# Selective scan: which engine multiplies by B and by C, and where dA and the states lie

## The chip, the core and the metric

The kernel runs on one core of one Trainium2 chip. The metric is the device time of one execution in microseconds (us). Five engines work side by side, each on its own in-order queue of instructions: PE (TensorE, matmuls; PEld is its weight load), DVE (VectorE), ACT (ScalarE), POOL (GpSimd) and SP (SyncE, which here issues all DMA transfers). An engine's instruction can wait for semaphores that other engines' instructions raise; whatever is queued behind it on the same engine waits too. SBUF is the on-chip working memory, PSUM the memory into which TensorE writes.

## The reference, cut to what matters

The input x is two images of 96 channels by 128 x 128 pixels. A block of four selective scans (Mamba) over the pixels in four orders, a quantised feed-forward layer, a 3 x 3 convolution and a second feed-forward layer follow each other; the change touches only the scans. For each of four directions, with 192 inner channels and 16 states per channel:

```python
xz = x @ in_w.T;  xc, z = split(xz)
xc = silu(conv4(xc) + conv_b)                   # causal, 4 taps, per channel
dt_raw, Bm, Cm = split(xc @ xproj_w.T)          # 6, 16 and 16 columns
dt = softplus(dt_raw @ dt_w.T + dt_b)
A = -exp(A_log)
def step(h, t):                                 # over 16384 positions
    dA = exp(dt_t[:, :, None] * A)
    h = dA * h + dt_t[:, :, None] * B_t[:, None, :] * u_t[:, :, None]
    y = einsum('bds,bs->bd', h, C_t)
    return h, y
y = (ys + Dp * xc) * silu(z)
out = y @ outp_w.T
```

## The kernel before, in words

For each of the two images (batches) `normalize` does a layer norm and writes the image to DRAM in row order (`xnr`) and column order (`xnc`), `mamba` does the four scans, and `ffn_and_conv` does the rest. Only `mamba` and the constants change.

`mamba` takes two directions at a time (a row order and a column order, forward for `pi` = 0 and backward for `pi` = 1), so that 2 x 192 = 384 channels fill three groups `g` of 128 partitions; group 1 holds 64 channels of each direction. Positions are cut into 32 pieces of T = 512. One pair of directions and one piece is a step: 2 x 32 = 64 steps per batch, 128 in all. In a step each group goes through the 16 states two at a time: 3 x 8 = 24 units (g, s) per step, 3072 in all.

A unit does this. TensorE broadcasts two rows of B over the partitions into the PSUM tile `bc` (L282, one-hot weights times three bf16 parts that sum to the float32 row). ScalarE makes `da` = exp(dt x A), one instruction per state (L285). VectorE multiplies dt x u (`dtu`) by the broadcast B inside `bc` (L290) and runs two scans h = da x h + b (L293), which start from the last states of the piece before, kept in `hst`. ScalarE copies the last columns of `h` to `hst` (L297). GpSimd multiplies `h` by two rows of C, `cs` (L299), which a DMA has broadcast from DRAM (`c_rows`, L274). TensorE adds the two products into the PSUM tile `y` by matmuls with an identity (L301).

After a group's eighth unit `finish` adds the skip Dp x xc to y on VectorE (L308), multiplies by the gate `sz` on GpSimd (L309), and behind groups 1 and 2 projects (L314 to L324) and adds the result to `acc`.

What a step needs beforehand is made during the step before by the generator `prologue`, one piece behind each unit from the third on: the loads of the input rows, the convolution folded into the input projection (L182), SiLU (L206, L211), the row products for C (L218, written to DRAM as `cd`) and for B and dt (L228), the split of B into bf16 parts, and for each group softplus in a numerically careful form: ScalarE |x|, relu(x), exp (L249 to L252), VectorE q (L255), ScalarE ln (L257), and on GpSimd q, ln, dt and dtu (L258 to L262).

The order on ScalarE's queue is the order in which the program is written (`manual_schedule`). On the other engines a scheduler orders the instructions when the program is built. Tiles come from pools with a fixed number of buffers; a tile that takes a buffer again waits for all readers of the tile that had it. PSUM holds two `bc` (two banks each), one `y` and three `misc`.

Of the kernel before, what the change touches and what calls it, by code (L numbers as in the profile page):

```python
# [1 line left out]

# [29 lines left out]
AHEAD = 3  # L32
DTO = 96
# [3 lines left out]
def tile_metaformer(ctx: ExitStack, tc: tile.TileContext, a: dict, out: bass.AP):  # L37
# [21 lines left out]
    bdw = const("bdw", (128, 2, NG, DTO + 2 * RK))  # L59
    cw = const("cw", (128, 2, NG, 2 * S))  # L60
    dtw = const("dtw", (2 * RK, 2, NG * 128))
    dtb = const("dtb", (128, 2, NG))
    dskip = const("dskip", (128, 2, NG))
# [4 lines left out]

    amat = cpool.tile([128, 2, NG, S], F32, name="amat")
    sel = cpool.tile([96, S, 2, 128], BF16, name="sel")  # L70
# [3 lines left out]
    with tc.tile_pool(name="prep", bufs=1) as pp, tc.tile_pool(name="prep_ps", bufs=2, space=PSUM) as pps:  # L74
# [4 lines left out]
        onehot = pp.tile([96, 2, S], F32, name="onehot")  # L79
        nc.sync.dma_start(onehot, a["onehot"])  # L80
        for d in range(2):
            nc.vector.tensor_copy(sel[:, :, d, :], onehot[:, d, :, None].broadcast_to((96, S, 128)))
# [75 lines left out]
    def mamba(acc, xnr, xnc):  # L158

        with ExitStack() as st:  # L160
            pool = lambda n, bufs, **kw: st.enter_context(tc.tile_pool(name=n, bufs=bufs, **kw))
            io, one, two, gen = pool("io", 2), pool("one", 1), pool("two", 2), pool("gen", 6)
            ps_bc, ps_y, ps_m = (pool(n, k, space=PSUM) for n, k in (("ps_bc", 2), ("ps_y", 1), ("ps_m", 3)))
# [21 lines left out]
            def prologue(pi, i, d):  # L185

                rev = pi == 1
                lo = L - (i + 1) * T if rev else i * T
                src = []
                for n, dram in (("xa", xnr), ("xb", xnc)):  # L190
                    t = io.tile([C, T + 3], F32, name=n)
                    if i == 0:
                        nc.gpsimd.memset(t[:, T : T + 3] if rev else t[:, 0:3], 0.0)
                        nc.sync.dma_start(t[:, 0:T] if rev else t[:, 3 : T + 3], dram[:, lo : lo + T])
                    else:
                        nc.sync.dma_start(t, dram[:, lo : lo + T + 3] if rev else dram[:, lo - 3 : lo + T])
                    src.append(t[:, ::-1] if rev else t)
                yield
                d["xc"], d["sz"], d["dt"], d["dtu"] = [], [], [], []
                ps = []  # L200
                for g in range(NG):
                    ps.append(inproj(pi, g, lambda dd, k, lo, hi: inx[:, dd, k, lo:hi], src, (0, 1, 2, 3)))
                    yield
                for g in range(NG):
                    xc = gen.tile([128, T], F32, name="xc")
                    nc.scalar.activation(xc, ps[g], AF.Silu, bias=convb[:, pi, g : g + 1])  # L206
                    d["xc"].append(xc)
                for g in range(NG):
                    z = inproj(pi, g, lambda dd, k, lo, hi: inz[:, dd, lo:hi], src, (3,))
                    sz = gen.tile([128, T], F32, name="sz", bufs=5)  # L210
                    nc.scalar.activation(sz, z, AF.Silu)  # L211
                    d["sz"].append(sz)
                nc.scalar.preload_act_table_set("natural_log_exp_and_others")
                yield

                ps = misc()
                for g in range(NG):
                    nc.tensor.matmul(ps[0 : 2 * S, :], cw[:, pi, g, :], d["xc"][g], start=g == 0, stop=g == NG - 1)  # L218
                crow = one.tile([2 * S, T], F32, name="crow")
                nc.scalar.copy(crow, ps[0 : 2 * S, :])  # L220
                d["cd"] = rows_d.tile([2 * S, T], F32, name="cd")
                nc.sync.dma_start(d["cd"], crow)
                yield


                ps = misc()
                for g in range(NG):
                    nc.tensor.matmul(ps[0 : DTO + 2 * RK, :], bdw[:, pi, g, :], d["xc"][g], start=g == 0, stop=g == NG - 1)  # L228
                parts = two.tile([96, T], BF16, name="parts")
                nc.scalar.copy(parts, ps[0:96, :])  # L230
                rest = one.tile([96, T], F32, name="rest")
                nc.vector.tensor_tensor(rest, ps[0:96, :], parts, ALU.subtract)
                dtr = one.tile([2 * RK, T], F32, name="dtr")
                nc.scalar.copy(dtr, ps[DTO : DTO + 2 * RK, :])
                yield
                mid = one.tile([96, T], BF16, name="mid")
                nc.gpsimd.tensor_copy(mid, rest)
                nc.vector.tensor_copy(parts[32:64, :], mid[32:64, :])
                nc.gpsimd.tensor_tensor(parts[64:96, :], rest[64:96, :], mid[64:96, :], ALU.subtract)
                d["parts"] = parts  # L240
                yield


                for g in range(NG):
                    ps = misc()
                    nc.tensor.matmul(ps, dtw[:, pi, g * 128 : (g + 1) * 128], dtr, start=True, stop=True)
                    bias = dtb[:, pi, g : g + 1]
                    e = one.tile([128, T], F32, name="e")
                    nc.scalar.activation(e, ps, AF.Abs, bias=bias)  # L249
                    dt = gen.tile([128, T], F32, name="dt", bufs=4)  # L250
                    nc.scalar.activation(dt, ps, AF.Relu, bias=bias)  # L251
                    nc.scalar.activation(e, e, AF.Exp, scale=-1.0)  # L252
                    yield
                    q = one.tile([128, T], F32, name="q")
                    nc.vector.tensor_scalar(q, e, 1.0, 1.0, ALU.add, ALU.subtract)  # L255
                    ln = one.tile([128, T], F32, name="ln")
                    nc.scalar.activation(ln, e, AF.Ln, bias=1.0)  # L257
                    nc.gpsimd.tensor_tensor(q, e, q, ALU.subtract)  # L258
                    nc.gpsimd.tensor_tensor(ln, ln, q, ALU.add)  # L259
                    nc.gpsimd.tensor_tensor(dt, dt, ln, ALU.add)  # L260
                    dtu = gen.tile([128, T], F32, name="dtu", bufs=4)
                    nc.gpsimd.tensor_tensor(dtu, dt, d["xc"][g], ALU.mult)  # L262
                    d["dt"].append(dt)
                    d["dtu"].append(dtu)
                    yield

            def c_rows(d, g, s):

                cs = gen.tile([128, 2, T], F32, name="cs", bufs=4)
                for half in range(2) if g == 1 else (slice(None),):  # L270
                    rows = slice(half * 64, half * 64 + 64) if g == 1 else half
                    at = s + S * (half if g == 1 else g // 2)
                    n = 64 if g == 1 else 128
                    nc.sync.dma_start(cs[rows], d["cd"][None, at : at + 2, :].broadcast_to((n, 2, T)))  # L274
                return cs

            def inputs_of(pi, d, g, s):

                bp = ps_bc.tile([128, 2, T], F32, name="bc")
                for j in range(2):  # L280
# [229 lines left out]
```

## Time and profile before

| | us |
|---|---|
| median of 3 runs | 18649.57 |
| lowest and highest | 18648.17 and 18655.98 |
| the profiled execution | 18639.52 |
| its span | 18637.7 |
| VectorE busy | 12812.0 (69%) |
| GpSimd busy | 10041.0 (54%) |
| ScalarE busy | 6766.3 (36%) |
| DMA, queue q1 | 1725.11 MB, 29.9% of 16 engines' time |
| TensorE's mean granted clock | 0.864 |

The profile page comes from one execution. Its groups name a line, an engine, an operation, out<-in, the shape and the count, then the busy time in us and the mean of one in ns, and behind the bar the idle time of the engine just before these instructions and what ended most of it. A line of waits reads: who waited, for whom, us in total, times, longest. A line of the timeline reads: start in us, duration in us, engine, line, operation, names, shape, count of merged instructions, and in brackets the idle time before. A line of stretches gives for each stretch the busy time of every engine with the number of instructions, the granted clock, the share of the DMA engines and GB/s.

### The profile page before, as it was taken

What the parts mean: (1) busy time and instruction counts of PE and PEld (TensorE: products, weight loads), DVE (VectorE), ACT (ScalarE), POOL (GpSimd) and SP (SyncE); (2) the same over time, 40 slices, a digit from 0 to 9 for tenths busy, and PEclk for the clock granted to TensorE, in tenths of its full rate; (3) what the DMA queues carried; (4) which work ended last, traced back from release to release, by engine and by line L of the source; (5) the groups of instructions that cost most, each with busy time, mean ns of one, the idle gap of its engine ahead of it and who ended that gap; (6) DMA issues with size and microseconds to landing.
All of it is one profiled execution on the core that took longest, in us unless ns stands there. A gap on an engine that the chain in (4) does not pass through costs nothing. (4 is left out here: it accounts for less than half of the span.)

```text
span 18637.7 us, 119806 instructions
## 1 busy us (share of the span) xinstructions
PE 14287.1 (77%) x33424; PEld 5080.7 (27%) x33424; DVE 12812.0 (69%) x12267; ACT 6766.3 (36%) x13205; POOL 10041.0 (54%) x5412
## 2 busy tenths in 40 slices
PE   6777777777777777777767777777787777777777
PEld 2222222222222222223322222222222222222233
DVE  4777777777777777753347777777777777777533
ACT  2433333343333433422223433333333334334222
POOL 2666666666666666630026666666666666666300
PEclk7888998899988888877778889988888888888777
DMA  2333333333333333310023333333333333333100
GB/s 87 109 105 108 108 107 108 105 108 108 107 106 106 106 106 106 107 55 6 6 85 106 108 106 108 108 107 106 106 107 107 104 107 106 108 106 106 54 6 6
DMA packets 511015, 1732.76 MB, mean 93 GB/s; under 512 B 75612, under 2 KB 76988, under 8 KB 505640
## 3 DMA queue, kind: packets, MB, share of 16 engines
q1 hardware_dynamic: 510344, 1725.11, 29.9%
q8 instruction: 263, 4.31, 0.1%
q14 instruction: 408, 3.34, 0.1%
HBM read 1678.68 MB, written 46.14 MB: 93 GB/s over the span
## 5 line engine op out<-in xcount | busy, mean ns | idle before, releaser
L299 POOL TENSOR_TENSOR hc<-h,cs 128x1024 f32<-128x1024 f32 x3072 | 7245.3, 2362 | 5219.9 <-DVE h L293 3434.5
L301 PE MATMUL y<-hc,ident 128*128 128x512 f32 x12288 | 7260.5, 722 | 2487.3 <-POOL hc L299 2456.2
L293 DVE TENSOR_TENSOR_SCAN h<-da,hst,bc 128x512 f32<-128x512 f32 x5952 | 7218.0, 1262 | 211.0 <-ACT da L285 72.9
L290 DVE TENSOR_TENSOR bc<-dtu,bc 128x1024 f32<-128x1024 f32 x3072 | 3685.8, 1219 | 2206.1 <-PE bc L282 2198.5
L301 PEld LDWEIGHTS y<-hc,ident 128*128 128x128 f32 x12288 | 2534.1, 224 | 6549.6 <-POOL hc L299 4297.4
L285 ACT ACTIVATE da<-dt,amat 128x512 f32<-128x512 f32 x6144 | 4080.7, 712 | 1.5
L297 ACT COPY hst<-h 128x2 f32<-128x2 f32 x3072 | 586.0, 191 | 7922.3 <-DVE h L293 7922.1
L282 PE MATMUL bc<-parts,sel 96*128 96x512 bf16 x6144 | 1970.8, 396 | 571.7 <-DVE h L293 568.4
L416 POOL TENSOR_TENSOR acc<-acc,y 96x512 f32<-96x512 f32 x128 | 147.0, 1148 | 2158.8 <-DVE y L415 2158.8
L282 PEld LDWEIGHTS <-sel 96*128 96x128 bf16 x6144 | 598.6, 102 | 2583.7 <-issue 2521.4
L182 PE MATMUL misc<-xa,inx 96*128 96x512 f32 (+1 forms) x2048 | 1054.8, 611 | 64.0 <-issue 32.2
L182 PE MATMUL misc<-xb,inx 96*64 96x512 f32 (+1 forms) x2048 | 1047.6, 610 | 0.3 <-ACT dt L251 0.3
L308 DVE SCALAR_TENSOR_TENSOR yg<-xc,dskip,y 128x512 f32<-128x512 f32 x384 | 285.3, 743 | 745.8 <-PE y L301 745.8
L309 POOL TENSOR_TENSOR yg<-yg,sz 128x512 f32<-128x512 f32 x384 | 485.5, 1264 | 543.9 <-DVE yg L308 486.8
L431 PE MATMUL pc<-pad,kw 96*96 96x512 f32 x1152 | 663.0, 699 | 48.2 <-DVE pad L129 48.2
L126 PE MATMUL pr<-sd,bcast_w 128*96 128x128 f32 x2048 | 450.1, 390 | 313.5 <-DVE sd L123 309.5
L114 ACT ACTIVATE sq<-xm 96x512 f32<-96x512 f32 x256 | 161.0, 629 | 1202.6 <-DVE xm L112 1161.1
L211 ACT ACTIVATE sz<-misc 128x512 f32<-128x512 f32 x384 | 229.3, 597 | 996.7 <-POOL yg L309 656.3
L260 POOL TENSOR_TENSOR dt<-dt,ln 128x512 f32<-128x512 f32 x384 | 490.9, 1278 | 20.2
L259 POOL TENSOR_TENSOR ln<-ln,q 128x512 f32<-128x512 f32 x384 | 485.5, 1264 | 30.1
L262 POOL TENSOR_TENSOR dtu<-dt,xc 128x512 f32<-128x512 f32 x384 | 486.6, 1267 | 27.8
L258 POOL TENSOR_TENSOR q<-e,q 128x512 f32<-128x512 f32 x384 | 484.7, 1262 | 9.6 <-DVE q L255 9.6
(88 smaller groups left out, 9731.6 us busy)
## 6 DMA issues: line engine op xcount, KB each, us to landing
cs<-cd SPq DMA_DIRECT2D x2048, 512.0 KB, 3.7
cs<-cd SPq DMA_DIRECT2D x2048, 256.0 KB, 3.9
xa<-xnr SPq DMA_DIRECT2D x124, 193.1 KB, 3.4
xb<-xnc SPq DMA_DIRECT2D x124, 193.1 KB, 4.0
acc<-in_x_dram SPq DMA_DIRECT2D x16, 768.0 KB, 16.2
xnr<-xn SPq DMA_DIRECT2D x16, 768.0 KB, 4.3
xnc<-st SPq DMA_DIRECT2D x16, 768.0 KB, 4.6
out_dram<-acc SPq DMA_DIRECT2D x64, 192.0 KB, 2.1
```

The costliest lines, as they stand in the source:

```text
L182: nc.tensor.matmul(ps[rows, :], w(PAIRS[pi][d], k, lo, hi), src[d][:, k : k + T], **se)
L259: nc.gpsimd.tensor_tensor(ln, ln, q, ALU.add)
L260: nc.gpsimd.tensor_tensor(dt, dt, ln, ALU.add)
L262: nc.gpsimd.tensor_tensor(dtu, dt, d["xc"][g], ALU.mult)
L282: nc.tensor.matmul(bp[:, j, :], w, d["parts"], start=True, stop=True)
L285: nc.scalar.activation(da[:, j, :], d["dt"][g], AF.Exp, scale=amat[:, pi, g, s + j : s + j + 1])
L290: nc.vector.tensor_tensor(bp, d["dtu"][g][:, None, :].broadcast_to((128, 2, T)), bp, ALU.mult)
L293: nc.vector.tensor_tensor_scan(h[:, j, :], da[:, j, :], bp[:, j, :], 0.0 if i == 0 else hst[:, g, s + j : s + j + 1], ALU.mult, ALU.add,)
L297: nc.scalar.copy(hst[:, g, s : s + 2], h[:, :, T - 1])
L299: nc.gpsimd.tensor_tensor(hc, h, cs, ALU.mult)
L301: nc.tensor.matmul(y, ident, hc[:, j, :], start=s + j == 0, stop=s + j == S - 1)
L431: nc.tensor.matmul(pc, kw[:, t, :], rows, start=t == 0, stop=t == 8)
```

## The change

B and C rows now come together. One row product (`bcw`) gives dt, B and C; `rows` writes the 64 rows of B and C, interleaved, to DRAM as `bcd`, and `bc_rows` broadcasts four rows (two of B, two of C) per unit by DMA into the SBUF tile `bc`, of which there are five buffers. GpSimd multiplies `dtu` into the B part of `bc`, two units ahead of the scan (L289). ScalarE writes `da` into PSUM (three buffers of two banks); the scans read it there and write the states back in its place (L300); ScalarE copies the last columns from there (L304), and VectorE multiplies the states by the C part of `bc` (L306). The skip becomes a matmul with a diagonal matrix `dmat` that opens the sum `y`; VectorE multiplies y by the gate. `misc` has one PSUM buffer instead of three. ScalarE takes the convolution and the gate out of PSUM as they are, and SiLU runs once over all three groups of each. The prologue's pieces stand at fixed units of the step before (`at`), and projection and collection two and three units behind a group's end.

```diff
-AHEAD = 3
-DTO = 96
+ROWS_AHEAD = 3
+AHEAD = 2
+BY_POOL = ()
+BCO = 32
+NBC = 4 * S
...
+        for pi in range(2):
+            for g in range(NG):
+                nc.vector.tensor_scalar_mul(dmat[:, pi, g, :], ident, dskip[:, pi, g : g + 1])
...
-            io, one, two, gen = pool("io", 2), pool("one", 1), pool("two", 2), pool("gen", 6)
-            ps_bc, ps_y, ps_m = (pool(n, k, space=PSUM) for n, k in (("ps_bc", 2), ("ps_y", 1), ("ps_m", 3)))
+            io, one, two, gen = pool("io", 2), pool("one", 1), pool("two", 2), pool("gen", 4)
+            ps_w, ps_y, ps_m = (pool(n, k, space=PSUM) for n, k in (("ps_w", 3), ("ps_y", 1), ("ps_m", 1)))
...
+                def conv(g):
+                    ps = inproj(pi, g, lambda dd, k, lo, hi: inx[:, dd, k, lo:hi], src, (0, 1, 2, 3))
+                    if g == 0:
+                        d["xc"] = two.tile([128, NG, T], F32, name="xc")
+                    nc.scalar.activation(d["xc"][:, g, :], ps, AF.Identity, bias=convb[:, pi, g : g + 1])
+
+                def gate(g):
+                    ps = inproj(pi, g, lambda dd, k, lo, hi: inz[:, dd, lo:hi], src, (3,))
+                    if g == 0:
+                        d["sz"] = two.tile([128, NG, T], F32, name="sz")
+                    nc.scalar.copy(d["sz"][:, g, :], ps)
+
+                def silu():
+                    for t in (d["xc"], d["sz"]):
+                        nc.scalar.activation(t, t, AF.Silu)
+                    nc.scalar.preload_act_table_set("natural_log_exp_and_others")
+
+                def rows():
+
+                    ps = misc()
+                    for g in range(NG):
+                        nc.tensor.matmul(
+                            ps[0 : BCO + NBC, :], bcw[:, pi, g, :], d["xc"][:, g, :], start=g == 0, stop=g == NG - 1
+                        )
+                    d["rows"] = one.tile([BCO + NBC, T], F32, name="rows")
+                    nc.scalar.copy(d["rows"], ps[0 : BCO + NBC, :])
+                    d["bcd"] = rows_d.tile([NBC, T], F32, name="bcd")
+                    nc.sync.dma_start(d["bcd"], d["rows"][BCO:, :])
...
+                def dt_in(g):
+                    ps = misc()
+                    nc.tensor.matmul(ps, dtw[:, pi, g * 128 : (g + 1) * 128], d["rows"][0 : 2 * RK, :], start=True, stop=True)
...
+                    nc.scalar.activation(d["e"], ps, AF.Abs, bias=bias)
...
+                    nc.scalar.activation(dt, ps, AF.Relu, bias=bias)
+                    nc.scalar.activation(d["e"], d["e"], AF.Exp, scale=-1.0)
...
+                def dt_ln(g):
+                    d["q"] = one.tile([128, T], F32, name="q")
+                    nc.vector.tensor_scalar(d["q"], d["e"], 1.0, 1.0, ALU.add, ALU.subtract)
+                    d["ln"] = one.tile([128, T], F32, name="ln")
+                    nc.scalar.activation(d["ln"], d["e"], AF.Ln, bias=1.0)
+
+                def dt_q(g):
+                    nc.gpsimd.tensor_tensor(d["q"], d["e"], d["q"], ALU.subtract)
+
+                def dt_log(g):
+                    nc.gpsimd.tensor_tensor(d["ln"], d["ln"], d["q"], ALU.add)
+
+                def dt_sum(g):
+                    nc.gpsimd.tensor_tensor(d["dt"][g], d["dt"][g], d["ln"], ALU.add)
+
+                def dt_u(g):
+                    dtu = gen.tile([128, T], F32, name="dtu")
+                    nc.gpsimd.tensor_tensor(dtu, d["dt"][g], d["xc"][:, g, :], ALU.mult)
...
+                at = [(0, load), (9, silu), (10, rows)]
+                at += [(k, partial(conv, g)) for g, k in enumerate((2, 3, 4))]
+                at += [(k, partial(gate, g)) for g, k in enumerate((5, 6, 8))]
+                for g, k in enumerate((11, 14, 18)):
+                    for m, f in ((0, dt_in), (1, dt_ln), (2, dt_q), (3, dt_log), (3, dt_sum), (4, dt_u)):
+                        at.append((k + m, partial(f, g)))
+                return sorted(at, key=lambda p: p[0])
+
+            def bc_rows(d, g, s):
+
+                bc = gen.tile([128, 2, 2, T], F32, name="bc", bufs=5)
...
+                    src = d["bcd"][None, at : at + 4, :].broadcast_to((n, 4, T))
+                    nc.sync.dma_start(bc[rows].rearrange("p s k t -> p (s k) t"), src)
+                return bc
+
+            def inputs_of(pi, d, g, s, bc):
+
+                b = bc[:, :, 0, :]
+                nc.gpsimd.tensor_tensor(b, d["dtu"][g][:, None, :].broadcast_to((128, 2, T)), b, ALU.mult)
+                da = ps_w.tile([128, 2, T], F32, name="da")
                 for j in range(2):
                     nc.scalar.activation(da[:, j, :], d["dt"][g], AF.Exp, scale=amat[:, pi, g, s + j : s + j + 1])
-                return bp, da
+                return da
+
+            def scans(i, d, g, s, bc, da):
+                b, c = bc[:, :, 0, :], bc[:, :, 1, :]
+                by_pool = (g, s) in BY_POOL
+                h = b if by_pool else da
                 for j in range(2):
                     nc.vector.tensor_tensor_scan(
-                        h[:, j, :], da[:, j, :], bp[:, j, :],
+                        h[:, j, :], da[:, j, :], b[:, j, :],
                         0.0 if i == 0 else hst[:, g, s + j : s + j + 1], ALU.mult, ALU.add,
                     )
                 nc.scalar.copy(hst[:, g, s : s + 2], h[:, :, T - 1])
-                hc = two.tile([128, 2, T], F32, name="hc")
-                nc.gpsimd.tensor_tensor(hc, h, cs, ALU.mult)
+                if not by_pool:
+                    nc.vector.tensor_tensor(c, h, c, ALU.mult)
+
+            def sums(s, y, bc):
                 for j in range(2):
-                    nc.tensor.matmul(y, ident, hc[:, j, :], start=s + j == 0, stop=s + j == S - 1)
+                    nc.tensor.matmul(y, ident, bc[:, j, 1, :], start=False, stop=s + j == S - 1)
...
+            def gated(pi, d, g, y):
                 t = one.tile([128, T], F32, name=f"yg{g}")
...
+                nc.vector.tensor_tensor(t, y, d["sz"][:, g, :], ALU.mult)
...
+            for k in range(total + 4):
+                n, u = divmod(k, nu)
+                if u == 0 and n + 1 < len(steps):
+                    for m, f in prologue(*steps[n + 1], state[n + 1]):
+                        later(k + m, f)
+                fetch(k + ROWS_AHEAD)
+                prepare(k + AHEAD)
+                for f in todo.pop(k, ()):
+                    f()
+                if k >= total:
+                    continue
+                (pi, i), d, (g, s) = steps[n], state[n], units[u]
+                scans(i, d, g, s, bc[k], da.pop(k))
+                if s == 0:
+                    if k > 0:
+                        pn = (k - 1) // nu
+                        gated(steps[pn][0], state[pn], units[k - 1 - pn * nu][0], y)
+                    y = ps_y.tile([128, T], F32, name="y")
+                    nc.tensor.matmul(y, dmat[:, pi, g, :], d["xc"][:, g, :], start=True, stop=False)
...
+                    sums(s, y, bc.pop(k))
+                if s == S - 2 and g > 0:
+                    later(k + 2, project, pi, d, g)
+                    later(k + 3, collect, pi, i, d, g)
```

In the built program VectorE's queue repeats every step like this (s5a and s5b are the two scans of unit 5, m5 its product with C, q the softplus piece, G the gate product, A and W the collections behind groups 1 and 2; units are counted from 0 in each step):

```
s0a s0b m23 s1a s1b m0 G s2a s2b m1 s3a s3b W s4a s4b m2 s5a s5b m3 s6a s6b m4
s7a m5 s7b s8a m6 s8b m7 s9a m8 G s9b s10a s10b m9 m10 s11a s11b q m11
s12a s12b m12 s13a s13b m13 q s14a s14b m14 s15a s15b m15 s16a s16b m16
s17a s17b G m17 s18a s18b A s19a s19b s20a q m18 s20b s21a m19 s21b s22a m20 s22b
s23a m21 s23b m22
```

On GpSimd's queue b(k) is the product of unit k with B; around the three softplus parts the order is: b(11) q b(12) ln dt dtu b(13) b(14) q ln b(15) dt dtu b(16) ... b(20) q b(21) ln dt dtu b(22) b(23).

## The prediction

> **What bounds the kernel now.** I read the page first, then the scan tiles, the stretches, the list of waits and two pieces of the order of time.
>
> ```profile
> span 18637.7 us, 119806 instructions
> PE 14287.1 (77%) x33424; PEld 5080.7 (27%) x33424; DVE 12812.0 (69%) x12267; ACT 6766.3 (36%) x13205; POOL 10041.0 (54%) x5412
> ...
> L299 POOL TENSOR_TENSOR hc<-h,cs 128x1024 f32<-128x1024 f32 x3072 | 7245.3, 2362 | 5219.9 <-DVE h L293 3434.5
> L293 DVE TENSOR_TENSOR_SCAN h<-da,hst,bc 128x512 f32<-128x512 f32 x5952 | 7218.0, 1262 | 211.0 <-ACT da L285 72.9
> L290 DVE TENSOR_TENSOR bc<-dtu,bc 128x1024 f32<-128x1024 f32 x3072 | 3685.8, 1219 | 2206.1 <-PE bc L282 2198.5
> L285 ACT ACTIVATE da<-dt,amat 128x512 f32<-128x512 f32 x6144 | 4080.7, 712 | 1.5
> ...
> cs<-cd SPq DMA_DIRECT2D x2048, 512.0 KB, 3.7
> ```
>
> No engine is full. The y sums of batch 0 start from 331.3 to 8157.1 and of batch 1 from 9634.4 to 17475.6 (matmuls that read tile hc): 7826 + 7841 = 15667 us for 128 steps of 24 units, 122.4 us a step. The other 2971 us (layer norms, feed-forward) the change doesn't touch; with the 1.8 us by which the profiled execution (18639.5) exceeds its span that is 2973. The profiled execution is 10 us under the median, 18649.6.
>
> ```profile
> 3000.00:4000.00 1000.00, 783.82 (x1714) 267.45 (x1713) 752.64 (x670) 391.61 (x770) 626.09 (x335) 0.89 0.35 107
> ...
> DVE bc L290 <- PE bc L282: 2198.5, 1158, 6.9
> DVE yg L308 <- PE y L301: 745.8, 318, 7.5
> ```
>
> Columns of the first line: PE, PEld, DVE, ACT, POOL busy, clock, DMA share, GB/s. VectorE works 0.753 x 122.4 = 92 us of a step and idles 30. It idles for the broadcast matmul of B and for y, both delayed in TensorE's queue. So what counts is not busy time but who waits in a queue; those waits I must count for the new order.
>
> ```profile
> 3006.85 1.23 DVE L290 TENSOR_TENSOR bc<-dtu,bc 128x1024 f32<-128x1024 f32 x1 [0.91 <-PE bc L282]
> 3007.75 1.99 PE L301 MATMUL y<-hc,ident 128*128 128x512 f32 x4
> 3008.21 2.45 DVE L293 TENSOR_TENSOR_SCAN h<-da,hst,bc 128x512 f32<-128x512 f32 x2
> 3010.70 0.19 ACT L297 COPY hst<-h 128x2 f32<-128x2 f32 x1 [3.30 <-DVE h L293]
> 3010.80 1.33 ACT L285 ACTIVATE da<-dt,amat 128x512 f32<-128x512 f32 x2
> ```
>
> Prices: independent VectorE instructions overlap (two scans 2.45, so 1.19 apart; two L290 elsewhere take 2.33, 1.12 apart). A scan that needs the L290 before it starts 1.36 after it, 0.13 after its end. ScalarE follows a scan 0.04-0.05 after its end. Exponentials are 0.62 apart. Four y matmuls take 1.99, 0.46 apart.
>
> **Parts with one answer.** Gone from TensorE: 48 bf16 passes and one of two row products (6 passes) a step; new: 6 skip passes. About 152 fp32 passes x 0.46 = 70 us of a step, so no bound. VectorE loses rest (0.66) and parts (0.28), and a product moves behind the scan. GpSimd keeps one 2.36 product a unit, 24 x 2.36 + 12 x 1.27 = 72 us. ScalarE gets plain copies in place of SiLU (0.69 and 0.57), plus one SiLU block: two table loads (1.28) and two 1536-column SiLUs, from 128 and 512 columns (0.37, 0.68) about 0.82 ns a column, 1.44 each: 5.4 us. Set-up is small: six scaled identities replace two 1.22 us copies. SP issues as many broadcasts, each twice as large.
>
> **VectorE's own queue.** 48 x 1.19 + 24 x 1.12 + three q at 0.83 + three gated at 0.64 + collects 0.67 and 1.18 = 90.3 us. In the built order 17 second scans stand right behind their first and now wait for it (both write one PSUM tile): 17 x 0.2 = 3.4. Five products stand right behind their own scans and wait for the hst copy, which reads the same tile: scan 1.255 + 0.05 + 0.19 + 0.04 instead of 1.19, 5 x 0.35 = 1.75. Together 95.4, and this is the floor. [...]
>
> **The waits that are added.** The exponentials of unit u+2 go into the da buffer of u-1 (three buffers), so they wait for product u-1; the hst copy of u stands behind them and behind the prologue piece of unit u in ScalarE's fixed order; product u waits for hst. From one product's end to the scan after next's release: 0.05 + 0.71 + 0.1 + 0.71 + 0.05 = 1.6 (the 0.1 between dependent exponentials no row shows; it lies between -0.09, the overlap above, and VectorE's 0.13, nearer the latter). [...] I walk one steady step from product to product, m17 of one to m17 of the next; every start is the latest of its releasers:
>
> m17 to m22: the third dt piece's matmul waits for the collect that frees the only misc buffer, ScalarE's three dt steps (1.9) follow, then q, and m18 stands behind q: 9.95. GpSimd's b(21) stands behind its q (1.27 + 2.36 after VectorE's q): 4.9. b(22) stands behind ln, dt, dtu (3 x 1.27): 6.1. Then 4.05 and 2.95. Sum 27.95.
> m22 to m1: VectorE alone, 3.7 + 3.7 + 4.35 = 11.75.
> m1 to m4: m2 waits for hst(2), behind conv(0)'s evacuation, whose eight passes (3.8) wait for the collect: 1.12 + 1.39 + 1.19 + 1.27 + 3.8 + 0.69 + 0.3 = 9.75. conv(1) waits for that evacuation, with sums(2) inside it in TensorE's queue: 7.5. conv(2): 6.6. Sum 23.85.
> m4 to m8: chain product, exponentials, scan, product: 1.22 + 1.6 + 1.19 = 4.0, twice; then 2.95 and 3.5 (hst behind exponentials and gate piece). Sum 14.45.
> m8 to m10: SiLU: 1.22 + 1.5 + 5.4 + 0.25 = 8.35; rows piece 3.5. Sum 11.85.
> m10 to m13: hst(11) and q behind dt_in(0): 5.45. b(12) stands behind GpSimd's q: 1.27 + 2.36, then scans to product 2.95: 6.65. b(13) behind ln, dt, dtu: 6.15. Sum 18.25.
> m13 to m17: q(1) stands ahead of scan 14 and waits for the Exp behind unit 16's exponentials: 1.22 + 1.5 + 1.9 + 0.83 + 2.9 = 8.35. Then b(15) stands behind GpSimd's ln, which waits for ScalarE's Ln behind exponentials that wait for m14: 1.22 + 1.5 + 0.63 + 1.27 + 2.36 + 2.95, with hand-overs 10.0. b(16) behind dt and dtu 4.9; 4.35. Sum 27.6.
>
> One step: 27.95 + 11.75 + 23.85 + 14.45 + 11.85 + 18.25 + 27.6 = 135.7 us, against 122.4. Total 128 x 135.7 + 2973 = 20343, say 20350.
>
> **Costs with two ends.** Scan with da and h in PSUM: never seen; L290 in PSUM shows no extra, the two scan forms differ by 0.06 (1.203 first step, 1.262), so 1.255 +/- 0.06: +/- 2.9 us a step, +/- 370 us. Dependent exponentials: about 14 on the path, -0.19 to +0.03: -340 to +50 us. A broadcast of 1 MB: 512 KB land in 3.7; the start of batch 0 moved four of them at 344 to 397 GB/s (2.6 us a MB at best), the loads of x at 250 GB/s with all queues full (4.2). So 24 take 63 to 101 us, no bound, and one lands after 5.0 (taken, as it is the same broadcast) to 5.8. Five buffers turn: sums 2.1, landing 5.0, GpSimd 2.36; behind m20 to m22 that leaves 1.2 us to spare, so 5.8 costs nothing.
>
> **Rivals.** (1) Faster: GpSimd runs ahead, that is b(12), b(13), b(15), b(16), b(21), b(22) are ready when their scans come. Price: 2.6 + 2.1 + 5.95 + 0.85 + 2.95 = 14.4 us less, 121.3 a step: 18500. It decides only if it recovers 13.3 of the 14.4. For it: GpSimd has 72 us of work in a step. Against: the built order puts those six behind q, ln, dt, dtu. Its limit, all waits hidden, is 95.4 a step: 15184.
> (2) Slower: broadcasts land late. The longest landing before was 6.7 for 512 KB; with 2.1 for the second half 8.8, and two turns of the ring lose 2.5 each: 140.7 a step, 20980. For it: doubled bytes. Against: the share was 0.35.
> (3) Slower: TensorE's clock falls. From m1 to m4 16.4 us are TensorE's; the feed-forward stretches run at 0.73-0.75, mamba at 0.89. At 0.64 it costs 6.4 us: 142.1 a step, 21160. Against: TensorE gets less to do in longer steps.
> (4) The waits only trade places and the step stays at 122.4: 18640.
>
> **How the numbers follow.** My walk 58%, (1) 18%, (2) 11%, (3) 10%, (4) 3%. The likeliest gives 20350, on its own 19600 to 20900 by the ends above. The range 18600 to 21300 takes in (2), (3) and the part of (1) in which GpSimd recovers some but not all; it leaves out (1) proper and about 2% above. Faster by over 0.2% (about what a measurement can tell): 18%; within: 3%; slower: 79%.
>
> **What would show it.** In the profile after: VectorE at about 70% of mamba or less; products (L306) waiting for the hst copy (L304), and scans (L300) idle before them on GpSimd's b (L289) and on exponentials (L292), some 40 us a step together; gaps of 8 us or more between products near q, conv and SiLU; DMA near 0.65. If scans wait for nothing and VectorE is above 85%, the walk is wrong and (1) holds. If GpSimd waits long for DMA, it is (2). A scan far from 1.26, or exponentials not tied to products, would break the sum.

## The result, and the profile after

The changed kernel takes 20139.8 us (median of four runs, 20132.1 to 20156.0) against 18652.8 us for the kernel before on the same chip: a ratio of 1.080, 95% interval 1.078 to 1.082. The profiled execution took 20156.0 us. With the 2971 us outside the scans unchanged, a step is (20154.2 - 2971) / 128 = 134.2 us against 122.4.

From the page of the changed kernel: the span, the engines' busy times, the groups of the scan and the broadcasts.

```profile
span 20154.2 us, 110511 instructions
PE 13714.6 (68%) x27280; PEld 4754.4 (24%) x27280; DVE 12913.5 (64%) x12015; ACT 7203.8 (36%) x13205; POOL 9265.5 (46%) x4772
...
L300 DVE TENSOR_TENSOR_SCAN da<-da,hst,bc 128x512 f32<-128x512 f32 x5952 | 7648.7, 1287 | 2905.8 <-POOL bc L289 2206.4
L292 ACT ACTIVATE da<-dt,amat 128x512 f32<-128x512 f32 x6144 | 4248.4, 692 | 5735.4 <-DVE bc L306 5636.2
L306 DVE TENSOR_TENSOR bc<-da,bc 128x1024 f32<-128x1024 f32 x3072 | 3738.9, 1217 | 1422.7 <-ACT hst L304 1406.1
...
bc<-bcd SPq DMA_DIRECT2D x2048, 1024.0 KB, 4.7
bc<-bcd SPq DMA_DIRECT2D x2048, 512.0 KB, 7.8
```

VectorE has as much to do as before (12913 us against 12812), and every other engine but ScalarE has less. What grew is VectorE's idle time: 2906 us ahead of scans, 1423 ahead of products and 659 ahead of q, 39 us a step. By what ended each wait, the trace gives 18.0 us a step for b, 11.0 for the state copy, 4.5 for exponentials and 5.1 ahead of q. The same stretch as before, by the view of stretches (PE, PEld, DVE, ACT, POOL, clock, DMA share, GB/s):

```profile
3000.00:4000.00 1000.00, 686.01 (x1223) 228.85 (x1224) 699.88 (x600) 383.71 (x708) 527.84 (x268) 0.82 0.63 192
```

VectorE works 70% of it instead of 75%. The list of waits says for whom it waits, and that GpSimd in turn waits for broadcasts:

```profile
POOL bc L289 <- DMA bc<-bcd: 3650.7, 1280, 9.8
...
DVE da L300 <- POOL bc L289: 2299.4, 1259, 6.3
```

The order of time of VectorE, first at units 2 and 3, then from unit 13 to unit 15, shows the kinds of wait that the prediction counted:

```profile
3041.70 1.23 DVE L306 TENSOR_TENSOR bc<-da,bc 128x1024 f32<-128x1024 f32 x1 [2.06 <-ACT hst L304]
3044.46 2.62 DVE L300 TENSOR_TENSOR_SCAN da<-da,hst,bc 128x512 f32<-128x512 f32 x2 [1.54 <-ACT da L292]
...
3103.25 0.43 DVE L249 TENSOR_SCALAR q<-e 128x512 f32<-128x512 f32 x1 [3.19 <-ACT e L244]
3103.59 2.61 DVE L300 TENSOR_TENSOR_SCAN da<-da,hst,bc 128x512 f32<-128x512 f32 x2
3106.43 1.22 DVE L306 TENSOR_TENSOR bc<-da,bc 128x1024 f32<-128x1024 f32 x1 [0.23 <-ACT hst L304]
3113.38 2.62 DVE L300 TENSOR_TENSOR_SCAN da<-da,hst,bc 128x512 f32<-128x512 f32 x2 [5.73 <-POOL bc L289]
3116.23 1.22 DVE L306 TENSOR_TENSOR bc<-da,bc 128x1024 f32<-128x1024 f32 x1 [0.23 <-ACT hst L304]
```

The product of unit 2 waits for the state copy, which stands behind the convolution's evacuation on ScalarE; the scan after it waits for exponentials that wait for a product; q waits for ScalarE; unit 15's scans wait for b. Of the 18.0 us a step for b, 15.0 stand ahead of the scans of units 12, 13, 15, 16, 21 and 22, whose b followed a softplus piece on GpSimd at once, without a wait for a DMA; 2.2 stand ahead of scans whose b had itself waited for a broadcast.

### The profile page after: what moved, and what is told of

Same layout as the page of the kernel before. It is cut to its first block, busy times and chain, and to the rows that moved or that the text cites. A ratio compares the mean times of both kernels' runs of the same rounds, so it can differ in the third digit from the quotient of the medians.

```text
span 20154.2 us, 110511 instructions
## 1 busy us (share of the span) xinstructions
PE 13714.6 (68%) x27280; PEld 4754.4 (24%) x27280; DVE 12913.5 (64%) x12015; ACT 7203.8 (36%) x13205; POOL 9265.5 (46%) x4772
## 4 chain that ended last, share of the span: by engine, by line
PE 22%; POOL 19%; DVE 19%; issue 17%; DMA 15%; ACT 7%; SPq 1%; POOLq 0%; ACTq 0%; DVEq 0%
DMA bc<-bcd 15%; POOL bc L289 13%; DVE da L300 9%; PE y L310 8%; PE misc L185 6%; DVE bc L306 6%; PE pc L466 2%; ACT da L292 2%; POOL ln L257 2%; PE pr L129 2%; PE pm L113 2%; POOL dt L260 2%; DVE sd L126 1%; POOL dtu L264 1%; POOL q L254 1%
## 5 line engine op out<-in xcount | busy, mean ns | idle before, releaser
L310 PE MATMUL y<-bc,ident 128*128 128x512 f32 x12288 | 7877.8, 777 | 3656.9 <-DVE bc L306 3656.5
L300 DVE TENSOR_TENSOR_SCAN da<-da,hst,bc 128x512 f32<-128x512 f32 x5952 | 7648.7, 1287 | 2905.8 <-POOL bc L289 2206.4
L289 POOL TENSOR_TENSOR bc<-dtu,bc 128x1024 f32<-128x1024 f32 x3072 | 7190.2, 2349 | 4721.2 <-DMA bc<-bcd 3650.7
L310 PEld LDWEIGHTS y<-bc,ident 128*128 128x128 f32 x12288 | 2707.3, 237 | 8764.9 <-DVE bc L306 6180.7
L306 DVE TENSOR_TENSOR bc<-da,bc 128x1024 f32<-128x1024 f32 x3072 | 3738.9, 1217 | 1422.7 <-ACT hst L304 1406.1
L386 PE MATMUL y<-xc,dmat 128*128 128x512 f32 x768 | 643.2, 933 | 1105.8 <-DVE yg L318 1105.8
L304 ACT COPY hst<-da 128x2 f32<-128x2 f32 x3072 | 476.5, 155 | 2460.6 <-DVE da L300 2459.2
L209 ACT ACTIVATE xc<-misc,convb 128x512 f32<-128x512 f32 x384 | 263.9, 687 | 1653.0 <-PE misc L185 1653.0
L325 PE MATMUL misc<-yg,gmat 128*96 128x512 f32 x1024 | 646.2, 718 | 194.1 <-ACT dt L243 192.5
L466 PE MATMUL pc<-pad,kw 96*96 96x512 f32 x1152 | 663.8, 700 | 48.2 <-DVE pad L132 48.2
L241 ACT ACTIVATE e<-misc,dtb 128x512 f32<-128x512 f32 x384 | 259.2, 675 | 782.6 <-PE misc L238 776.1
```

The source lines that it names most:

```text
L289: nc.gpsimd.tensor_tensor(b, d["dtu"][g][:, None, :].broadcast_to((128, 2, T)), b, ALU.mult)
L300: nc.vector.tensor_tensor_scan(h[:, j, :], da[:, j, :], b[:, j, :], 0.0 if i == 0 else hst[:, g, s + j : s + j + 1], ALU.mult, ALU.add,)
L306: nc.vector.tensor_tensor(c, h, c, ALU.mult)
L310: nc.tensor.matmul(y, ident, bc[:, j, 1, :], start=False, stop=s + j == S - 1)
L386: nc.tensor.matmul(y, dmat[:, pi, g, :], d["xc"][:, g, :], start=True, stop=False)
L466: nc.tensor.matmul(pc, kw[:, t, :], rows, start=t == 0, stop=t == 8)
```

## The experiments

The theory under test: VectorE has about 95 us of work in a step, and the other 39 us are waits made by the order of in-order queues. GpSimd makes b behind softplus pieces that wait for others, and ScalarE makes the state copy behind prologue pieces while the product waits for it. The rivals: broadcasts land too late (A), operands in PSUM slow VectorE (B), TensorE or GpSimd is too slow (C, D). TensorE's order is the scheduler's in every run. All runs, with the step from each profiled span as above:

| run | us | to the kernel before | step, us |
|---|---|---|---|
| changed kernel | 20139.8 | 1.080 [1.078, 1.082] | 134.2 |
| e1 states in SBUF | 21393.3 | 1.147 [1.145, 1.150] | 143.9 |
| e2 copy first | 18914.3 | 1.014 [1.012, 1.016] | 124.6 |
| e3 deeper ring | 19522.2 | 1.047 [1.045, 1.049] | 129.3 |
| e4 b further ahead | 20165.7 | 1.081 [1.080, 1.083] | 134.3 |
| e5 GpSimd in order | 18487.4 | 0.992 [0.990, 0.994] | 121.2 |
| e6 and VectorE in order | 17943.8 | 0.962 [0.961, 0.964] | 117.0 |
| e7 all in order, copy first | 17641.2 | 0.946 [0.944, 0.948] | 114.6 |
| e8 half the broadcast | 18331.5 | 0.983 [0.981, 0.984] | 120.0 |
| e9 as e6, b late again | 19856.6 | 1.065 [1.063, 1.067] | 131.9 |
| e10 as e6, half the broadcast | 18228.7 | 0.978 [0.976, 0.979] | 119.2 |
| e11 as e7, product before copy | 16676.2 | 0.895 [0.893, 0.896] | 107.1 |
| e12 as e11, states in SBUF | 17931.3 | 0.962 [0.960, 0.963] | 116.9 |

### First four: one edit each, the scheduler free

e1 puts the states back into SBUF:

```diff
-                h = b if by_pool else da
+                h = b
```

> Undoes one part alone: the scans write the states over b in SBUF instead of over the exponentials in PSUM; everything else is as in the changed kernel. Theory (a step of 134.1 us is VectorE's own 95 us plus waits that in-order queues and the shared PSUM tile make): the product no longer waits for ScalarE's copy of the last states (1406 us in all) and the exponentials of unit u+2 wait for the second scan of unit u-1 instead of its product. A step falls to 105 to 115 us: 24 x (2.61 + 1.22 + 0.13) = 95, q, gates and sums 5 to 7, and 5 to 13 left for GpSimd's late b: 16400 to 17700 us. Rival A (broadcasts of 1 MB land too late): PSUM plays no part, the time stays within 2% of 20140. Rival B (VectorE is slower because its operands lie in PSUM, 1.29 against 1.255 us a scan): 6144 x 0.035 = 215 us less at most, 19900 or more.

All three were wrong: 21393 us, 6% above the changed kernel (rival B's "19900 or more" takes that in, but it had argued for a gain). The product no longer waits (93 us instead of 1423), but it became longer, 1839 ns on the mean. In the order of time two kinds stand side by side:

```profile
3034.48 1.23 DVE L306 TENSOR_TENSOR bc<-bc 128x1024 f32<-128x1024 f32 x1
3039.16 2.46 DVE L300 TENSOR_TENSOR_SCAN bc<-da,hst,bc 128x512 f32<-128x512 f32 x2 [3.46 <-POOL bc L289]
3041.66 3.15 DVE L306 TENSOR_TENSOR bc<-bc 128x1024 f32<-128x1024 f32 x1
```

The first made GpSimd's dtu piece (from 3034.59) take 2.24 us instead of 1.27, the second ran inside five b's in a row (3036.79 to 3049.32). The scheduler also moved nearly every product behind its own scans in this run, so the 1250 us are not the place of the states alone; e12 settles that.

e2 moves the prologue's pieces behind the unit's own work in the program's text, which is ScalarE's order:

```diff
-                for f in todo.pop(k, ()):
-                    f()
...
                 scans(i, d, g, s, bc[k], da.pop(k))
+                for f in todo.pop(k, ()):
+                    f()
```

> Moves the pieces of the next tile's prologue behind the unit's scans, state copy and product in program order; no instruction is added or taken away. Theory: on ScalarE the state copy of a unit no longer stands behind the evacuations of conv and gate, SiLU and the dt pieces, so the long gaps between products from unit 1 to 4 (9.5, 7.3, 6.2 us), 8 to 9 (8.3) and 14 to 15 (9.8) shrink, but the pieces then stand ahead of the exponentials of the unit after: 4 to 10 us a step, 18850 to 19650 us. Rival A (late broadcasts) and rival C (GpSimd's b is what the step waits for, 2206 us in the table of groups): ScalarE's order plays no part, within 1% of 20140.

18914 us, as the theory had it. By the same walk from product to product, units 1 to 4 take 16.1 us on the mean of the steps instead of 23.3, 13 to 17 22.9 instead of 26.5 and 17 to 22 25.3 instead of 28.9; 10 to 13 lose 4.8 to b, and SiLU (8 to 10) stays at 11.6. That is 9.6 us a step, but not by ScalarE's order alone: the scheduler also put 12 instead of 5 products directly behind their own scans, q of the second group a unit later, and b(15) and b(16) ahead of softplus pieces that they had followed. With VectorE's and GpSimd's orders held, the same edit is worth 2.3 us (e7 against e6, below).

e3 asks for broadcasts one unit earlier:

```diff
-ROWS_AHEAD = 3
+ROWS_AHEAD = 4
...
-                bc = gen.tile([128, 2, 2, T], F32, name="bc", bufs=5)
+                bc = gen.tile([128, 2, 2, T], F32, name="bc", bufs=6)
```

> Broadcasts are asked for four units ahead instead of three, with six buffers instead of five; nothing else is edited. Theory: they land in 4.7 us and are used two units (11 us) later, so the step hardly changes: 19900 to 20200 us. Rival A (late broadcasts; GpSimd waits 3651 us for DMAs): most of the 5.7 us that a unit has over VectorE's own work goes where it waits for b: 5 us a step or more, 19500 us or less.

19522 us lies between both, 22 us above the rival's bound. But the scheduler's order of VectorE changed too (36 instead of 31 scans a step that start without depending on the instruction in front), and on GpSimd b(12) came ahead of q, so this run does not tell a later landing from the order.

e4 splits the b product from the exponentials, makes it three units ahead and asks for broadcasts four units ahead, in the same five buffers:

```diff
-ROWS_AHEAD = 3
+ROWS_AHEAD = 4
+B_AHEAD = 3
...
+                prepare_b(k + B_AHEAD)
                 prepare(k + AHEAD)
```

> GpSimd makes b three units ahead of the scan instead of two, broadcasts are asked for four units ahead, in the same five buffers; the exponentials stay two units ahead and VectorE's program order is the same. Rival 1 of the prediction put all of GpSimd's lateness at 14.4 us a step: 18300 us, 18500 with the waits that take its place. Theory: GpSimd's queue holds the same dt chain in the same place, one unit earlier, and products that waited for b wait for ScalarE's exponentials next: 3 to 9 us a step, 19000 to 19750 us. Rival A: five buffers hold the broadcast back to the sums of unit k-1, so they land no earlier for their use: within 1% of 20140.

20166 us, no change, as A had it; but the trace shows another reason than the DMA. GpSimd's order of time at the first softplus part, first in the changed kernel, then in e4:

```profile
3086.17 1.27 POOL L254 TENSOR_TENSOR q<-e,q 128x512 f32<-128x512 f32 x1 [7.89 <-DVE q L249]
3087.40 2.35 POOL L289 TENSOR_TENSOR bc<-dtu,bc 128x1024 f32<-128x1024 f32 x1
3089.70 1.26 POOL L257 TENSOR_TENSOR ln<-ln,q 128x512 f32<-128x512 f32 x1
```

```profile
3089.03 1.27 POOL L255 TENSOR_TENSOR q<-e,q 128x512 f32<-128x512 f32 x1 [8.15 <-DVE q L250]
3090.25 2.35 POOL L362 TENSOR_TENSOR bc<-dtu,bc 128x1024 f32<-128x1024 f32 x1
3092.56 1.26 POOL L258 TENSOR_TENSOR ln<-ln,q 128x512 f32<-128x512 f32 x1
```

The scheduler orders GpSimd's queue itself, and put each b at the same place among the softplus pieces (b(15) even one piece later): GpSimd idles 8 us for VectorE's q, and b(12) behind it does not depend on q. So e4 had not moved what it meant to move.

### The queues in the order of the text

e5 takes the scheduler's freedom away on GpSimd, e6 on VectorE too, and e7 adds e2's edit:

```diff
-st.enter_context(tc.manual_schedule(engines={mybir.EngineType.Activation}))
+st.enter_context(tc.manual_schedule(engines={mybir.EngineType.Activation, mybir.EngineType.Pool}))
```

> GpSimd's queue takes the order in which the kernel's text names the instructions, as ScalarE's already does; VectorE's and TensorE's order is still the scheduler's. No instruction is added or taken away. Theory, sharpened by the run with b three units ahead (20166 us: the scheduler put the b's between the same dt pieces as before, so that run did not get b ahead of anything): VectorE waits for b because GpSimd's queue holds b(14) to b(17) behind dt pieces that wait for VectorE's q and ScalarE's logarithm. In the order of the text two b's more stand ahead of each such wait. The 54.8 us from the product of unit 10 to that of unit 18 fall to 40 to 46, those from 18 to 22 by 2 to 4: 10 to 18 us a step, 17800 to 18850 us. Rival A (broadcasts too late): the b's wait for DMA instead, 19600 us or more. Rival D (GpSimd's own speed, 2.35 us a b): no change of order helps, 19900 or more.

18487 us, inside the theory's range: 13 us a step, and from the product of unit 10 to that of 18 it is 42.4 us on the mean instead of 55.1. VectorE's order, still the scheduler's, changed as well (35 instead of 31 scans that do not depend on the instruction in front, q of the second group two units later), so e5 alone does not price GpSimd's order; e9 does. GpSimd's first q now follows b(15) instead of b(11); the order of time in e6, whose GpSimd queue is the same, shows the last two of these b's:

```profile
3089.66 2.34 POOL L289 TENSOR_TENSOR bc<-dtu,bc 128x1024 f32<-128x1024 f32 x1 [2.87 <-DMA bc<-bcd]
3094.33 2.35 POOL L289 TENSOR_TENSOR bc<-dtu,bc 128x1024 f32<-128x1024 f32 x1 [2.33 <-DMA bc<-bcd]
3096.63 1.27 POOL L254 TENSOR_TENSOR q<-e,q 128x512 f32<-128x512 f32 x1
```

This q waits for nobody any more: VectorE had started its part 9 us before (3087.62).

> As the run with GpSimd in the order of the text, and VectorE in that order too: the two scans of a unit, then its product. Theory: q is reached a little earlier and each product now stands directly behind its own scans, so each waits 0.23 us for the state copy, and where prologue pieces stand ahead of that copy on ScalarE (units 2 to 10) nothing is left to do meanwhile: about the time of the run with GpSimd alone, within 400 us of it. Rival D: 19900 or more.

17944 us, 544 less than e5 where I had allowed 400 either way. Scans idle 4 us for b in the whole run, by the same line of the table of groups that had 2206.

> GpSimd and VectorE in the order of the text, and the prologue's pieces behind the unit's scans, state copy and product (as in the run that moved them). Theory: both causes of the waits are gone. A unit is 2.61 + 0.23 + 1.14 = 3.98 us; 24 of them 95.5, q 1.2, gates 1.8, two sums 1.8 make 100.3 us; conv units 1.3 us longer each and 4 for SiLU on ScalarE: 107 to 113 us a step, 16650 to 17450 us. Rival A: 19000 or more. Rival C (TensorE: its clock falls and its 13715 busy us stand in the way): 18200 or more.

17641 us, 191 above the range, and 303 less than e6. The steady unit is 3.98 us as worked out, but the product still waits 2217 us for the state copy where a convolution's evacuation (up to 6.8 us), SiLU (3.4 us) or a softplus piece (up to 4.1 us) of the unit before is still running, and q takes 1.31 us on the mean instead of 0.43. Rival D had 19900 us or more for e5 and e6, rival C 18200 or more for e7; with these times both fall.

### Putting the late b back

e9 is e6 with GpSimd's order put back: the six b's stand between the softplus pieces again, where the scheduler had them. Against the other instructions the pieces move as well: on VectorE q of the second group stands one unit earlier and of the third two units later, on ScalarE each ln up to two units.

```diff
+                    if k // nu + 1 == len(steps) or k % nu not in (12, 13, 15, 16, 21, 22):
+                        b_of(k)
...
-                    for m, f in ((0, dt_in), (1, dt_ln), (2, dt_q), (3, dt_log), (3, dt_sum), (4, dt_u)):
-                        at.append((k + m, partial(f, g)))
+                    chain = [partial(f, g) for f in (dt_ln, dt_q, dt_log, dt_sum, dt_u)]
+                    chain.insert(3 if g == 1 else 2, partial(held, u))     # b(12), b(15), b(21)
+                    at += [(at_b, f) for f in chain + [partial(held, u + 1)]]
```

> The run with GpSimd and VectorE in the order of the text (117.0 us a step), with one thing put back: GpSimd's queue has the order that the scheduler gave it in the changed kernel, b(12), b(13), b(15), b(16), b(21) and b(22) between the pieces of the dt chains. No instruction is added or taken away, and VectorE's and ScalarE's orders stay but for the pieces of those chains. Theory (b made late by its place in GpSimd's queue): from the product of unit 10 to that of 18 back from 38.5 us towards the 54.8 of the changed kernel, from 18 to 22 from 16.7 towards 21.6: 12 to 20 us a step, 19450 to 20500 us. Rival A (broadcasts) and rival D (GpSimd's speed): the order of the same instructions costs nothing, 17800 to 18200 us.

19857 us: 1913 us more by the places of the six b's and the softplus pieces, with as many instructions of nearly the same lengths. Units 10 to 18 take 48.2 us on the mean (38.4 in e6), 18 to 22 22.3 (16.5). Behind q on VectorE the two waits of the prediction are back:

```profile
3037.13 0.42 DVE L249 TENSOR_SCALAR q<-e 128x512 f32<-128x512 f32 x1
3041.28 2.62 DVE L300 TENSOR_TENSOR_SCAN da<-da,hst,bc 128x512 f32<-128x512 f32 x2 [3.74 <-POOL bc L362]
3044.13 1.23 DVE L306 TENSOR_TENSOR bc<-da,bc 128x1024 f32<-128x1024 f32 x1 [0.23 <-ACT hst L304]
3047.49 2.62 DVE L300 TENSOR_TENSOR_SCAN da<-da,hst,bc 128x512 f32<-128x512 f32 x2 [2.14 <-POOL bc L362]
```

The two orders (e6, e9) differ by 14.9 us a step. Of that, 13.4 are VectorE's scans idle for b, all at the six units named (1740 us in the run against 21); so this cause is shown.

### The bytes

e8 and e10 broadcast only the rows of B, in the changed kernel and in e6:

```diff
-                    src = d["bcd"][None, at : at + 4, :].broadcast_to((n, 4, T))
+                    src = d["bcd"][None, at : at + 4 : 2, :].broadcast_to((n, 2, T))
...
-                    nc.vector.tensor_tensor(c, h, c, ALU.mult)
+                    nc.vector.tensor_tensor(c, h, b, ALU.mult)
```

> The changed kernel with the rows of B alone broadcast, 512 KB a unit instead of 1 MB; the product multiplies the states by b, so the multiplication by C is left out of what is computed, while each engine runs the same instructions on the same shapes. Theory (order of the queues): DMAs are not what the step waits for, 19800 to 20250 us. Rival A (broadcasts land late; GpSimd waits 3651 us for them): 19500 us or less.

> Half the broadcast again, since in the run that halved it the scheduler also changed both orders (GpSimd's b's came ahead of the dt pieces, VectorE's q two units later), so that its gain of 1800 us names no cause. Here GpSimd and VectorE are in the order of the text, so that only the bytes differ from the run in that order (17944 us): rows of B alone, 512 KB a unit, and the product multiplies by b, so the multiplication by C is left out of what is computed. Theory: 17700 to 17950 us. Rival A (broadcasts land late): 16900 us or less.

e8 came out at 18331 us, which looks like rival A to the letter. But its two queues have another order (GpSimd's q, ln and dt now follow b's that came ahead, VectorE's q stands two units later), so it changed two things. In e10 the order is held, and half the bytes cost 285 us instead of saving any. Neither side had expected a loss. The broadcasts of e10, the wait of GpSimd for them, and q:

```profile
bc<-bcd SPq DMA_DIRECT2D x2048, 512.0 KB, 3.7
bc<-bcd SPq DMA_DIRECT2D x2048, 256.0 KB, 3.9
```

```profile
POOL bc L289 <- DMA bc<-bcd: 4765.1, 2078, 6.5
```

```profile
L249 DVE TENSOR_SCALAR q<-e 128x512 f32<-128x512 f32 x384 | 706.7, 1840 | 145.5 <-ACT e L244 145.5
```

The broadcasts over 128 partitions land in 3.7 us instead of 4.6, the halves over 64 in 3.9 instead of 6.6, and GpSimd still waits 4765 us for them (4482 in e6): an engine that has nothing else to do waits for its next broadcast in both. q went from 0.50 to 1.84 us, 514 us of VectorE's time; that this is the 285 us is argued, not shown. Rival A falls in this order of the queues. In the order of the changed kernel no run varies the bytes alone; there the trace speaks against it, with 2.2 of 18.0 us a step of scans idle behind a b that waited for a broadcast.

### The best order, and what the place of the states is worth

e11 is e7 with the product ahead of the state copy in the text:

```diff
+                if not by_pool:
+                    nc.vector.tensor_tensor(c, h, c, ALU.mult)
                 nc.scalar.copy(hst[:, g, s : s + 2], h[:, :, T - 1])
-                if not by_pool:
-                    nc.vector.tensor_tensor(c, h, c, ALU.mult)
```

> The run with everything in order and the pieces behind the unit's work (17641 us, 114.6 us a step), and the product ahead of the state copy in the text: the copy waits for the product instead of the product for the copy. Theory: the product then waits for its own scan alone, and what ScalarE does meanwhile (conv 4.8, 0.7 and 1.6 us, SiLU 3.2, dt 3.7 a step) is hidden up to a unit's length: 24 x (2.61 + 0.1 + 1.14) = 92.4, q 1 to 3, gates 1.8, sums 1.9: 97 to 104 us a step, 15400 to 16300 us. Rival A (broadcasts, 1 MB in 3.9 us): 17000 or more. Rival C (TensorE's busy time, 85 us a step in that run, with loads 29): 17000 or more.

16676 us, a ratio of 0.895 to the kernel before: the parts of the change, unaltered, in another order beat both kernels. It stayed 376 us above the range, though below both rivals. The 3.9 us that rival A took for 1 MB was an estimate; in e11 these broadcasts landed in 4.7 us on the median, the halves over 64 partitions in 9.3. The groups of e11:

```profile
L300 DVE TENSOR_TENSOR_SCAN da<-da,hst,bc 128x512 f32<-128x512 f32 x5952 | 7667.0, 1288 | 1058.3 <-POOL bc L289 730.4 <-ACT hst L306 190.8 <-ACT da L292 22.3
...
L305 DVE TENSOR_TENSOR bc<-da,bc 128x1024 f32<-128x1024 f32 x3072 | 3762.1, 1225 | 198.1 <-DVE da L300 4.1 <-PE y L310 1.4
```

The product waits 198 us instead of 2220: with VectorE's and GpSimd's orders as in e7, this exchange is worth 965 us, 7.5 us a step, so the state copy ahead of the product is shown as the second cause. New is that scans wait again, 1058 us, mostly for b. In the trace, 560 of the 773 us that scans idle for b in all stand ahead of a b that had itself waited for a broadcast: in this shorter step the broadcasts do come near the bound. VectorE is busy 90% of the stretch from 3000 to 4000 us.

e12 is e11 with e1's line, so that both orders are held:

> One line apart from the run with the product before the state copy (16676 us): the states are written over b in SBUF instead of over the exponentials in PSUM. Both engines' orders are fixed, so that the place of the states is all that differs. In the first run of this kind the same product took 1.23 us while GpSimd stood still and 3.15 us while it made a b, 1.84 on the mean. Theory P (VectorE, when both its operands lie in SBUF, and GpSimd hold each other up): the product rises from 1.225 to 1.7 to 2.3 us, 3072 x 0.5 to 1.1 = 1500 to 3400 us, less 3072 x 0.15 = 460 for the scan pair (2.46 instead of 2.61): 17700 to 19600 us. Rival: the 3.15 us belonged to the order of that run; the product keeps 1.2 us, and the pair and GpSimd's and ScalarE's earlier release save some: 16000 to 16700 us.

17931 us, 1255 more than e11 (1.075 times). The product takes 2157 ns against 1225. The order of time of both engines in e12:

```profile
3003.76 2.34 POOL L289 TENSOR_TENSOR bc<-dtu,bc 128x1024 f32<-128x1024 f32 x1
...
3005.08 2.10 DVE L305 TENSOR_TENSOR bc<-bc 128x1024 f32<-128x1024 f32 x1
...
3006.07 2.25 POOL L257 TENSOR_TENSOR ln<-ln,q 128x512 f32<-128x512 f32 x1
```

GpSimd's b ends at 3006.10 and VectorE's product 1.08 later, at 3007.18; GpSimd's ln ends 1.14 after that, at 3008.32, and takes 2.25 instead of 1.27: in these rows each ends as if it had stood behind the whole of the other's instruction. Over the whole run the product takes 1.225 us where GpSimd stands still (380 of 3072) and 2.29 on the mean where it works. With the states in PSUM (e11) the product takes 1.225 us on the mean, and in the rows from 3000 to 3150 us 1.22 to 1.23 each, in the 29 that GpSimd works beside and in the 6 where it stands still. The scans in e12, one input of which is in PSUM, stay at 2.44 to 2.45 us a pair in the same rows, beside GpSimd or not. So the states in PSUM are what makes the product on VectorE cheap here, 1.225 us instead of 2.157; by what mechanism no run shows.

## Why the prediction was right, point by point

The predicted 20350 us stands against 20139.8; the profiled execution took 20156.0. The walk gave 135.7 us a step, and one step of the trace (3001.93 to 3136.06, from the product of unit 18 to the next one) takes 134.1.

| products | predicted | measured |
|---|---|---|
| 17 to 22 | 27.95 | 28.62 |
| 22 to 1 | 11.75 | 12.38 |
| 1 to 4 | 23.85 | 23.03 |
| 4 to 8 | 14.45 | 14.41 |
| 8 to 10 | 11.85 | 11.60 |
| 10 to 13 | 18.25 | 17.58 |
| 13 to 17 | 27.6 | 26.51 |

- The stretches came out between 1.1 us shorter and 0.7 longer than predicted, and in the sum these errors partly cancel. Single waits held too: the 9.95 us behind the third softplus piece measured 10.71, the 9.75 behind the convolution 9.48, the 8.35 of SiLU 8.33, the 10.0 of b(15) 9.80. e9 and e11 each took one of the two causes in hand, with nearly all else in place.
- Mis-sized terms: q was taken at 0.83 us, its mean before, and took 0.433; in its new place 380 of 384 meet no instruction of GpSimd. With it 10 to 11 came out at 4.75 instead of 5.45 and 13 to 14 at 7.59 instead of 8.35. A scan took 1.287 us, not 1.255 (a bound of 0.06 was given); the state copy 0.155, not 0.19; an exponential 0.692 instead of the 0.712 of before.
- "VectorE alone" between units 22 and 1 was short by 0.8 at unit 0, which waits for GpSimd's b; and the collection behind unit 18's scans waits 2 us for TensorE's projection, a wait that the prediction does not name.
- The price of dependence: two scans, the second waiting for the first, take 2.61 us against 2.45 before, 0.16 a pair: 0.12 because the second starts 0.03 to 0.04 after the first's end instead of 0.08 before it, the rest because a scan is longer. The prediction took 0.2.
- Rival (1) had the right price and the wrong condition. It said 14.4 us if the six b's were ready; with the b's ahead a step is 14.9 us shorter (e9 against e6), and in the changed kernel the scans of these six units idle 15.0 us a step, but the built order did not let the b's be ready.
- Rival (2), late broadcasts: the landing of the 512 KB pairs, 7.8 us, came near its 8.8, yet 15.0 of the 18.0 us for b stand behind softplus pieces, and with the order held half the bytes saved nothing (e10). The sign that I named for it, GpSimd waiting long for DMA, was a bad one: it waited 3651 us, and in e6's order 4482 us, and 4765 with half the bytes.
- Rival (3), TensorE's clock: it did fall, to 0.82 in the scans instead of 0.89, but stayed far from the 0.64 that the rival assumed, and it was 0.88 in e11, whose steps are shorter. Rival (4) fell with the time.

## What to carry to other kernels

Before moving work between engines, list for each in-order queue what stands ahead of the instruction that the busiest engine waits for; the wait that ends the step is found there, not in busy shares, and here could be summed to 1% before the run. When a scheduler orders the queues, compare its order in both programs before reading an experiment: here e4 and e8 would have named the wrong cause, and e2 the wrong price. An engine that waits long for a DMA is no proof that the DMA is late (here it waited 4482 us, and 4765 with half the bytes); hold the order and halve the bytes.

## What was not expected of the hardware

- VectorE and GpSimd hold each other up in e12, where VectorE's product reads both inputs from SBUF: the product takes 1.23 us alone, up to 3.18 beside GpSimd in the rows from 3000 to 3150 us and 2.157 on the mean of the run, GpSimd's 512-column pieces in these rows up to 2.25 instead of 1.27.
- q, with one input and its output in SBUF, can be stretched too: it takes 1.84 us on the mean in e10, 1.78 to 2.42 in the four rows from 3000 to 3150 us, all beside GpSimd. In the changed kernel, where 380 of 384 meet no instruction of GpSimd, it took 0.43.
- Halving a broadcast's bytes shortened its landing over 128 partitions only from 4.6 to 3.7 us (e6, e10).
- What e11 still loses, 107.1 us a step against about 96 of VectorE's own (it is busy 90% of the stretch), was not tested further. By its trace 6.0 us a step are scans idle for b, 4.4 of them behind a b that waited for a broadcast; whether a deeper ring of buffers would help there was not tried.
